# The first image's channel statistics shared between VectorE and ScalarE, and three early loads issued from another queue

## The chip, the core and the metric

One core of a Trainium2 chip runs the kernel. The metric is the device time of one execution in microseconds (us), the median of several. VectorE is called DVE in the profile, ScalarE is ACT, TensorE is PE (its weight loads PEld), GpSimd is POOL, and SyncE, which here only issues transfers, is SP.

## The reference, cut to what matters

The input `x` has shape (2, 512, 64, 64): two images of 512 channels. Two layers follow each other, each of the form `x = x + layer(_gn(x))`. The first is a deformable convolution (a projection by `in_w`, a depthwise 3x3 convolution with a layer norm and a GELU, offsets and masks from it, bilinear sampling, a projection by `out_w`), the second an attention layer with a batch norm at its end. Here only the first group norm matters:

```python
def _gn(v, G=32, eps=1e-5):
    B_, C_, H_, W_ = v.shape
    g = v.reshape(B_, G, C_ // G, H_, W_)
    m = jnp.mean(g, axis=(2, 3, 4), keepdims=True)
    s = jnp.var(g, axis=(2, 3, 4), keepdims=True)
    return ((g - m) / jnp.sqrt(s + eps)).reshape(v.shape)
```

Each image is thus read whole before anything of its first layer can start: mean and variance over 16 channels and all 4096 pixels.

## The kernel before, in words

The 512 channels are four blocks (`kb`, KB = 4) of 128 channels, one channel on each partition. An image's 4096 pixels are eight chunks (NCH = 8) of 512. The first layer goes over the 16 chunks of both images in turn (NSEQ = 16); the second layer follows when the first has ended.

**The head.** The four blocks of the first image are loaded into `img[0]` to `img[3]` (two of them lie in the room of `bt`, the other two in buffers called `img`), each block in two halves of 1 MB: the first half is issued by ACT, the second by SP (L649 and L650). Behind them SP issues the weights: `in_w` (L651), small vectors, `om_w`, `out_w`, `wv`, `wf`, and `edge` (L691). `image_stats(0)` (L703, called at L1148) then takes a `bn_stats` of each chunk of each block on DVE (L727), and a `bn_aggr` for each block (L729), which leave the mean and the variance of each channel in `mv`. `group_norm_steps` (L595) turns them into a scale and a bias for each channel: two small PE products with `gmat`, a few small DVE operations, and a square root on ACT (L611). Only then can `project(0)` normalize the first chunk into `xn` (L762) and multiply it by `in_w` (L772).

**The second image's statistics.** `image_stats(1)` is a generator that is advanced a step at a time between other work, by `more()`. It has room for three pieces of one chunk of one block each (256 KB): two in `early`, one in `xraw`. `refill()` (L710) issues loads for free room, on POOL (L714); the first three are issued at its first step, the others when a `bn_stats` has emptied a piece.

**The order after the head** is written out by hand (L1154 on, under `manual_schedule`): the instructions of an engine, and the transfers it issues, keep the order in which the code names them. On SP this is: eight stores of the projected first chunk (L780), then `border()` (L695), 16 stores of `edge` into the borders of both projected images (L698 with 68 rows, L699 with 64 rows), then two stores of `wc_part` (L1134, from `value_weights`, L1124), then the stores of the second projected chunk. `more()` at L1166, the first step of `image_stats(1)`, stands behind `border()` in the code. `wc_part` and the projected rows `xj` (L777, L778) share two buffers, so the first `xj` of the second chunk waits until the first `wc_part` has been stored. What stands outside the hand-written order (the loads, `image_stats(0)`) is placed by a scheduler that works with modelled times.

Of the kernel before, what the change touches and what calls it, by code (L numbers as in the profile page):

```python
# [10 lines left out]
F32 = mybir.dt.float32  # L11
I32 = mybir.dt.int32
AF = mybir.ActivationFunctionType
ALU = mybir.AluOpType
AX = mybir.AxisListType
# [3 lines left out]
P = 128  # L19
NB = 2  # L20
C = 512
KB = C // P
H = W = 64
S = H * W
# [7 lines left out]
CH = 512  # L32
NCH = S // CH
# [521 lines left out]
def window_path(  # L555
# [3 lines left out]
    nc = tc.nc  # L559
    x_v = t_in["x"].rearrange("n (cb p) h w -> n p cb (h w)", p=P)  # L560
# [34 lines left out]
    def group_norm_steps(mv, k, small, psum, result):  # L595

        p1 = psum.tile([P, CH], F32, tag="mm", name="gn_p1")
        nc.tensor.matmul(p1[:, : 2 * k], gmat, mv.rearrange("p k s -> p (k s)"), start=True, stop=True)
        yield
        gm = small.tile([P, k, 2], F32, name=f"gn_gm{k}")  # L600
        nc.vector.tensor_copy(gm.rearrange("p k s -> p (k s)"), p1[:, : 2 * k])
        d = small.tile([P, k], F32, name=f"gn_d{k}")
        nc.vector.tensor_sub(d, mv[:, :, 0], gm[:, :, 0])
        nc.vector.tensor_mul(d, d, d)
        yield
        p2 = psum.tile([P, CH], F32, tag="mm", name="gn_p2")
        nc.tensor.matmul(p2[:, :k], gmat, d, start=True, stop=True)
        yield
        var = small.tile([P, k], F32, name=f"gn_var{k}")
        nc.vector.tensor_add(var, gm[:, :, 1], p2[:, :k])  # L610
        nc.scalar.activation(var, var, AF.Sqrt, bias=eps)  # L611
        yield
        sc = small.tile([P, k], F32, name=f"gn_sc{k}")
        nc.vector.reciprocal(sc, var)
        bi = small.tile([P, k], F32, name=f"gn_bi{k}")
        nc.vector.scalar_tensor_tensor(bi, gm[:, :, 0], -1.0, sc, ALU.mult, ALU.mult)
        result += [sc, bi]
# [8 lines left out]
    with ExitStack() as l0:  # L626
# [3 lines left out]
        sm = l0.enter_context(tc.tile_pool(name="w0small", bufs=1))  # L630
        ps = l0.enter_context(tc.tile_pool(name="w0ps", bufs=4, space=PSUM))
# [11 lines left out]
        img = [bt.rearrange("p g q d -> p (g q d)")[:, h * S : (h + 1) * S] for h in range(2)]  # L643
# [59 lines left out]
        def image_stats(n):  # L703

            mv = sm.tile([P, KB, 2], F32, name="gn_mv")
            room = [early[:, 0], early[:, 1], io.tile([P, CH], F32, name="xraw")] if n else []
            pieces, ahead = deque((kb, h) for kb in range(KB) for h in range(NCH)), deque()


            def refill():  # L710
                while len(ahead) < 3 and pieces:
                    k2, h2 = pieces.popleft()
                    ahead.append(room[len(pieces) % 3])
                    nc.gpsimd.dma_start(ahead[-1], x_v[n, :, k2, h2 * CH : (h2 + 1) * CH])  # L714

            if n:
                refill()
                yield
            for kb in range(KB):
                st = sm.tile([P, NCH, 6], F32, name="gn_st")  # L720
                for h in range(NCH):
                    if n == 0:
                        t = img[kb][:, h * CH : (h + 1) * CH]
                    else:
                        refill()
                        t = ahead.popleft()
                    nc.vector.bn_stats(st[:, h, :], t)  # L727
                    yield
                nc.vector.bn_aggr(mv[:, kb, :], st.rearrange("p a b -> p (a b)"))  # L729
            yield  # L730
            result = []
            yield from group_norm_steps(mv, KB, sm, ps, result)
            sc, bi = result
            gn[n] = [sm.tile([P, KB], F32, name=f"gn_{k}{n}") for k in ("scale", "bias")]
            nc.vector.tensor_copy(gn[n][0], sc)
            nc.vector.tensor_copy(gn[n][1], bi)
# [400 lines left out]
        def output_bias():  # L1137
# [8 lines left out]
            yield  # L1146

        run(image_stats(0))  # L1148
        later, y, f = image_stats(1), Chain(sample, NSEQ), Chain(features, 2)

        def more():
            next(later, None)

        with tc.manual_schedule():  # L1154
# [59 lines left out]
            for i in range(NSEQ):  # L1214
# [11 lines left out]
                ahead, taps = (7, (9, 7, 6, 6)) if i else (0, (7, 7, 6, 6))  # L1226
# [8 lines left out]
    with ExitStack() as l1, tc.manual_schedule():  # L1235
# [78 lines left out]
        with ExitStack() as inner:  # L1314
            wk = inner.enter_context(tc.tile_pool(name="w1work", bufs=1))
            ps = inner.enter_context(tc.tile_pool(name="w1ps", bufs=1, space=PSUM))
# [562 lines left out]
            for n in range(NB):  # L1879
# [3 lines left out]
                for i in range(NCH // 2):  # L1883
                    if 0 < i < 3 or n and i == 0:
                        k = i + 1 if i else 1
# [164 lines left out]
```

## Time and profile before

| what | us |
|---|---|
| median of 3 runs (lowest, highest) | 3310.23 (3306.95, 3310.55) |
| the profiled execution's own time | 3315.49 |
| its span in the profile | 3313.6 |
| PE busy | 3154.1 (95%) |
| DVE busy | 2729.4 (82%) |
| ACT busy | 1343.0 (41%) |
| first normalization on ACT (L762) starts | 36.56 |
| first product with `in_w` on PE (L772) starts | 37.48 |

The profile is of one execution. In the timeline each row gives the start, the duration, the engine, the line, the operation, output and inputs, and in brackets the time for which the engine had been idle and what ended that. SPq and ACTq are the sequencers that issue transfers. In the chain of waits each piece is the work that ended last, in order of time. The table's last two rows say how long the core waits before its matrix work begins.

### The profile page before, as it was taken

The numbers are of one execution on the slowest core, as the hardware profiler recorded it, in microseconds if no ns is written. First come the engines' busy times: TensorE is split into PE (matmuls) and PEld (weight loads), VectorE is DVE, ScalarE is ACT, GpSimd is POOL, SyncE is SP. The second block draws the span as 40 slices with busy tenths as digits, with TensorE's granted clock in tenths as the row PEclk, the third lists the DMA queues.
The fourth block names the chain that finished last, engine by engine and source line by source line (L and its number), as shares of the span: only waits on it lengthen the run. The fifth ranks groups of instructions, "written<-read, shape, count | busy, mean of one in ns | idle before, by whom it ended". The sixth has DMA issues, their size and how long they took to land.

```text
span 3313.6 us, 38405 instructions
## 1 busy us (share of the span) xinstructions
PE 3154.1 (95%) x14207; PEld 2264.5 (68%) x14207; DVE 2729.4 (82%) x3907; ACT 1343.0 (41%) x1848; POOL 292.0 (9%) x420
## 2 busy tenths in 40 slices
PE   4899999999999899999999999999999999999993
PEld 2455556555655667787787877887777787787782
DVE  7999999999998678995876977968897796886875
ACT  2678887888786533203113112023311202203114
POOL 1100000000000001001001011000001101001022
PEclk9999999999999999999999999999999999999997
DMA  6345443444343368748657677657677758648689
GB/s 238 120 117 155 151 129 109 137 146 118 109 136 124 115 236 282 220 154 242 189 174 212 197 203 204 199 185 251 226 213 200 205 181 234 199 160 238 194 320 373
DMA packets 241236, 629.06 MB, mean 190 GB/s; under 512 B 28528, under 2 KB 45552, under 8 KB 240016
## 3 DMA queue, kind: packets, MB, share of 16 engines
q1 hardware_dynamic: 177952, 413.37, 37.8%
q0 software_dynamic: 51936, 179.86, 20.7%
q10 hardware_dynamic: 11152, 33.30, 2.7%
q8 instruction: 114, 1.87, 0.2%
q14 instruction: 82, 0.67, 0.1%
HBM read 406.61 MB, written 124.91 MB: 160 GB/s over the span
## 4 chain that ended last, share of the span: by engine, by line
PE 79%; DVE 10%; ACT 5%; DMA 3%; issue 1%; SPq 1%; POOL 0%; ACTq 0%; POOLq 0%; DVEq 0%
PE accy L1572 21%; PE accx L1572 16%; PE pa L976 7%; PE py L996 6%; PE pS L1454 6%; PE pq L772 6%; PE po L866 4%; PE pvy L1809 3%; PE pvx L1809 2%; PE pk L1890 2%; PE pb L957 2%; ACT bt L962 1%; DMA tot<-e 1%; DVE conv L806 1%; PE p_mean L822 1%
## 5 line engine op out<-in xcount | busy, mean ns | idle before, releaser
L1572 PE MATMUL accy<-tt,v 128*128 128x256 f32 x1944 | 579.0, 379 | 0.7 <-DVE ct L1638 0.6
L1459 ACT ACTIVATE e<-pS 128x1024 f32<-128x1024 f32 x256 | 248.6, 1021 | 748.5 <-PE pS L1454 744.2
L1572 PE MATMUL accx<-e,v 128*128 128x256 f32 x1728 | 453.3, 385 | 0.0
L1572 PE MATMUL accy<-e,v 128*128 128x256 f32 x1728 | 443.4, 379 | 0.0
L1572 PEld LDWEIGHTS accy<-tt,v 128*128 128x128 f32 x1944 | 368.7, 190 | 53.3 <-DVE tt L1530 2.2
L806 DVE SCALAR_TENSOR_TENSOR conv<-xn,L_conv_dw_w_sb,conv 128x504 f32<-128x504 f32 (+1 forms) x512 | 376.7, 744 | 30.5 <-ACT conv L798 14.7
L1572 PEld LDWEIGHTS accx<-e,v 128*128 128x128 f32 x1728 | 320.5, 190 | 116.3 <-issue 77.4
L1572 PEld LDWEIGHTS accy<-e,v 128*128 128x128 f32 x1728 | 328.3, 190 | 44.6
L1530 DVE TENSOR_TENSOR tt<-tt,e 128x512 f32<-128x512 f32 x432 | 298.8, 692 | 14.8
L1572 PE MATMUL accx<-tt,v 128*128 128x256 f32 x972 | 289.4, 379 | 1.3 <-DVE tt L1529 1.3
L1529 DVE TENSOR_TENSOR tt<-e 128x256 f32<-128x256 f32 x432 | 180.7, 418 | 133.0 <-PE accy L1572 131.0
L976 PEld LDWEIGHTS pa<-bt,patch 96*128 96x128 f32 x2048 | 248.3, 195 | 57.1 <-issue 39.2
L976 PE MATMUL pa<-bt,patch 96*128 96x128 f32 x2048 | 252.3, 280 | 7.5 <-issue 4.0
L1454 PE MATMUL pS<-q,keys 64*128 64x512 f32 x1024 | 255.5, 616 | 1.1 <-DVE vform L1827 0.8
L962 ACT COPY bt<-pb 96x1024 f32<-96x1024 f32 x120 | 226.0, 2024 | 52.6 <-PE pb L957 52.6
L772 PE MATMUL pq<-in_w,xn 128*128 128x512 f32 x512 | 234.1, 600 | 3.5 <-ACT xn L762 3.5
L996 PE MATMUL py<-dT,L_conv_out_w_sb 128*128 128x512 f32 x512 | 230.0, 593 | 0.0
L1577 ACT COPY u<-accx 128x256 f32<-128x256 f32 x54 | 20.1, 372 | 474.5 <-PE accx L1572 471.7
L866 PE MATMUL po<-om_w_pg,feat 128*128 128x432 f32 x512 | 210.3, 557 | 0.8 <-ACT feat L849 0.8
L987 ACT COPY dT<-pa 32x256 f32<-32x256 f32 x496 | 179.9, 363 | 67.8 <-PE pa L976 59.0
L1572 PEld LDWEIGHTS accx<-tt,v 128*128 128x128 f32 x972 | 184.4, 190 | 27.6 <-DVE tt L1529 2.5
L996 PEld LDWEIGHTS py<-dT,L_conv_out_w_sb 128*128 128x128 f32 x512 | 95.5, 190 | 114.3 <-issue 107.6
(289 smaller groups left out, 4386.7 us busy)
## 6 DMA issues: line engine op xcount, KB each, us to landing
v<-wv SPq DMA_DIRECT2D x420, 448.0 KB
tot<-e POOLq DMA_DIRECT2D x160, 512.0 KB, 6.8
patch<-xt SPq DMA_DIRECT2D x256, 192.0 KB
wv<-vform SPq DMA_DIRECT2D x48, 512.0 KB
v<-ww SPq DMA_DIRECT2D x54, 448.0 KB
wv<-vsum SPq DMA_DIRECT2D x48, 384.0 KB
xt<-xj SPq DMA_DIRECT2D x128, 128.0 KB
res<-in_x SPq DMA_DIRECT2D x64, 256.0 KB
```

Source lines behind the costliest of these rows:

```text
L772: nc.tensor.matmul(pq, xn[:, kb, 1 + 2 * t : 3 + 2 * t, :].rearrange("p r c -> p (r c)"), in_w[:, kb, :], start=(kb == 0), stop=(kb == KB ...
L806: nc.vector.scalar_tensor_tensor(dst, src, wt, dst, ALU.mult, ALU.add)
L866: nc.tensor.matmul(po[:, : 3 * GP], f[:, kb, t * P : (t + 1) * P], om_w[:, kb].rearrange("p a k g -> p (a k g)"), start=(kb == 0), stop=(k ...
L962: copy(bt[:SN].rearrange("s g q d -> s d (g q)")[:, d0 : d0 + 4, :], pb[:SN])
L976: nc.tensor.matmul(pa[:, p], xp[:SN, p, cb * P : (cb + 1) * P], bt[:SN, 4 * cb : 4 * cb + 4, PX * s + p, :], start=True, stop=True,)
L987: copy(dst, src)
L996: nc.tensor.matmul(py, out_w[:, kb, cb * P : (cb + 1) * P], dT[:, kb, :], start=(kb == 0), stop=(kb == KB - 1))
L1454: nc.tensor.matmul(p[:, a, :], keys[r, i, (2 * u + h) * P : (2 * u + h + 1) * P], c.q[r, qh, :], start=True, stop=True,)
L1459: nc.scalar.activation(e.rearrange("p a q -> p (a q)"), p.rearrange("p a q -> p (a q)"), AF.Exp)
L1529: nc.vector.tensor_sub(t[:, 0], x[:, 1], x[:, 3])
L1530: nc.vector.tensor_add(t[:, 1:3], t[:, 0].unsqueeze(1).to_broadcast([P, 2, HQ]), x[:, 0:3:2])
L1572: nc.tensor.matmul(out, v[:, blk, :], op, start=(first and g == 0), stop=(final and g == NG))
```

## The change

For the first image (n = 0) block 1 is left out of the loop on DVE. In its place ACT goes over the eight chunks of `img[1]` twice each: Identity with scale 1/4096, and Square with scale 4096^-0.5, both into scratch tiles in PSUM, with `accum_out`, which adds up each row of 512 values: 16 instructions give eight partial sums of the mean and eight of the mean square. Ahead of block 3's statistics DVE joins them: a sum over the eight parts, the square of the mean, and a subtraction. For the second image nothing of this applies; but its first three loads (256 KB each) are issued by SP in place of POOL, at the same place in the code: the first `more()`, behind `border()`.

```diff
                     k2, h2 = pieces.popleft()
                     ahead.append(room[len(pieces) % 3])
-                    nc.gpsimd.dma_start(ahead[-1], x_v[n, :, k2, h2 * CH : (h2 + 1) * CH])
+                    queue = nc.gpsimd if len(pieces) < KB * NCH - 3 else nc.sync
+                    queue.dma_start(ahead[-1], x_v[n, :, k2, h2 * CH : (h2 + 1) * CH])
 
             if n:
                 refill()
                 yield
+            by_scalar = 1 if n == 0 else KB
+            if n == 0:
+                acc = sm.tile([P, 2, NCH], F32, name="gn_acc")
+                for h in range(NCH):
+                    for k, (func, scale) in enumerate(((AF.Identity, 1.0 / S), (AF.Square, S ** -0.5))):
+                        p = ps.tile([P, CH], F32, tag="mm", name="p_sq")
+                        nc.scalar.activation(
+                            p, img[by_scalar][:, h * CH : (h + 1) * CH], func, scale=scale,
+                            accum_out=acc[:, k, h : h + 1]
+                        )
             for kb in range(KB):
+                if kb == by_scalar:
+                    continue
+                if n == 0 and kb == KB - 1:
+                    both = mv[:, by_scalar, :]
+                    nc.vector.tensor_reduce(both, acc, AX.X, ALU.add)
+                    nc.vector.tensor_mul(acc[:, 0, 0:1], both[:, 0:1], both[:, 0:1])
+                    nc.vector.tensor_sub(both[:, 1:2], both[:, 1:2], acc[:, 0, 0:1])
                 st = sm.tile([P, NCH, 6], F32, name="gn_st")
```

## Prediction

> **What bounds the kernel now.** I read the chain of waits of the first 120 us first, because the change touches nothing behind that. Columns: start, us, what.
>
> ```profile
> 1.66 17.45 DMA bt<-in_x
> 19.11 0.02 issue
> 19.14 2.49 DVE gn_st L727 x4
> 21.62 0.02 issue
> 21.65 0.38 DVE gn_mv L729
> 22.03 0.02 issue
> 22.05 4.86 DVE gn_st L727 x8
> 26.93 0.38 DVE gn_mv L729
> 27.34 4.86 DVE gn_st L727 x8
> 32.22 0.38 DVE gn_mv L729
> ...
> 71.88 4.94 DMA wvfc<-wc_part
> 76.82 0.02 issue
> 76.84 0.02 ACTq L778
> 76.86 0.04 issue
> 76.90 0.59 ACT xj L778
> 77.48 0.00 issue
> 77.48 0.02 ACTq L778
> 77.50 0.04 issue
> 77.54 0.59 ACT xj L778
> 78.13 0.54 ACT feat L832
> ```
>
> Two places matter. **The head**: from 19.14 to 32.60 DVE works without a break on blocks 1, 2 and 3; the end of that sets the first matrix product at 37.48. **The SP queue**: from 55.6 on the chain runs through the 16 border stores, then through the store of `wc_part`, whose landing at 76.8 frees the buffer for `xj`. ACT takes its work in order, so Square (L832) stands behind `xj`, and PE, which had run out of work at 71.2 (L772: 64.17 + 7.03), goes on only at 78.71. The timeline of SP shows what stands there:
>
> ```profile
> 69.37 1.92 SPq L698 DMA_DIRECT2D xt<-raw  x1
> 71.33 0.45 SPq L699 DMA_DIRECT2D xt<-raw  x1
> 71.88 2.34 SPq L1134 DMA_DIRECT2D wvfc<-wc_part  x2
> ```
>
> The hand-written order puts the three moved loads exactly between the last two of these rows. That SP keeps that order is seen in the trace: `edge` was ready for the border at 43.34 (L693: 42.92 + 0.42), SP sat waiting for `xj` 18.4 us between 44 and 55, and still issued all eight L780 before the first border store.
>
> **Part 1: transfers leave the head.** POOL issues the first pieces of the second image at 2.67 to 4.33, and in windows of 1 us its queue moves 0.79 MB between 5 and 18 us, beside the first image. From 18 to 25 us all queues together move about 0.415 MB per us, so 0.79 MB are 1.9 us. SP's queue had moved the second half of block 2 at 22.4 us; a release follows its last byte by about 1.4 us here (block 0's half: 11.2 and 12.67; block 1's: 17.5 and 19.11; block 3's: 25.1 and 26.4). So that half lands at 23.8 before and at 21.9 after; block 1's halves at 12.5 and 17.2, block 3's last at 24.5.
>
> **Part 2: DVE's chain.** Block 1's eight `bn_stats` and aggregate (5.3 us) go. What is late next is a load: DVE does block 0, then block 2's first half, then waits for its second half until 21.9. From there: four `bn_stats` 2.43, aggregate 0.41, end 24.74; the join; then block 3, which before began at 27.34. The join's operations have no row of their size: a reduction took 0.145 (L543, one column) to 0.277 (128 elements, L1787), a small subtraction 0.18 (L603), a small product 0.16, but 0.85 the first time (L604: one of 0.850, three near 0.161). Together 0.5 to 1.2. The slow first product is already in the chain at 33.69, so by these rows it would only move to the join; I take 0.5 net. Block 3 then starts at 25.24: **2.1 us earlier**. Ends: 2.6 if the join is hidden in a wait, 1.4 if it costs 1.2.
>
> **Part 3: ACT's new work.** Sixteen instructions of 128x512 with an accumulator into PSUM; no row shows just that. Square from SBUF to SBUF (L832) is 0.62, four in 2.19. With an accumulator there is L890: 1.15 for 1152 elements, and the reading of the accumulator (0.187) lets the next one start 1.15 after the first, so it hardly adds. Low end 0.55 each, high end the slowest row of this width (L798, 0.814) plus 0.187: 1.0 each. I take 0.62, by L832 and L890. Block 1's first half lands at 12.5, so eight end at 17.5, when the second half is there (17.2); all end at 22.4. DVE needs the sums at 24.74: covered by 2.3 us, and ACT had nothing else to do (idle 30.76 before L611 at 35.42). At 1.0 each ACT ends at 28.5, block 3 starts at 29.0 and the head is 1.7 us later than before. A table load took 1.283 (at 3.38, far ahead of the square root): another one would fall in the ACT idle time from 22.4 to 33. The Trainium skill speaks against this division of work (ScalarE: Activation LUTs, Rules for kernel authors: adding and multiplying belong on VectorE, and a switch of table sets is to be budgeted at some 2.7 us). With such a switch on the path the head would be 0.6 us later, in place of 2.1 earlier; the idle row says it is off the path.
>
> **Part 4: three loads on SP.** They stand in front of `wc_part`, so whatever they take goes onto the chain at 71.88. Nothing of it is hidden: PE is idle 7.5 us there, and Square's input was ready at 69.13. Issue alone is 3 x 0.45 = 1.35. By the bytes: 0.79 MB at 0.415 is 1.9; at the rate at which the two `wc_part` stores moved (0.52 MB in some 1.6 us) 2.4. By the slow border rows (1.92 for one) it would be 5.8, by the slowest (2.35) 7.05. Low end 0. I take **1.9**, because the queue is in order and bytes wait there, and a 128-row tile is spread like `wc_part`, not like the slow 68-row L698. One rule of the Trainium skill bears on that (DMA: Bandwidth & Descriptors, in the part on the number of engines: the largest divisor up to 16 of the row count): 68 rows would run on 4 engines and 64 on 16, which fits L698 beside L699; by it the loads pay like L699, and the sum would use 1.35 to 1.9. The same page (Issuing engines are not separate DMA queues) holds that the issuing engine matters only for issue time; by that, Part 4 would cost 1.35.
>
> The loads then land at about 75.5, 76.2 and 76.8 on the old clock, and DVE reads them at 77.39, 77.99 and 78.58: no wait, with 1.8 us to spare. If they came 2 us later, DVE would wait that long, and pieces 3 to 5 with it; `rstd` follows at 85.3 from the PE side, and DVE's own work ends at 85.89, so up to 1.9 us of that vanish behind part 4's delay. POOL loses three issues of 0.55 in its idle time: nothing. Weights behind the image arrive 1.9 us earlier (`in_w` landed at 28.98, PE needs it at 35.4): nothing late there. `edge` finishes moving at about 38.8, lands near 40.2, and DVE's L693 would come at 40.8: covered by 0.6.
>
> **Sum.** -2.1 in the head, +1.9 on SP: -0.2 us. From 78.7 to 111 the chain is PE, then ACT and DVE, all released by this point, so the sum goes through unchanged. Against the profiled execution (span 3313.6, time 3315.49, so 1.9 outside the span, untouched) that is 3315.3; that execution is 5.3 above the median of the runs, so against the median: **3310.0**.
>
> **Rivals.**
> A. *The loads do not stand in the way*: SP issues them directly behind the first image's loads, or the other transfer engines take them beside the border stores. Part 4 is 0, the sum -2.1: 3308.1. Against it: SP's order in the trace.
> B. *The SP queue becomes the price* (slower): each load is issued at the pace of L698, 1.77 to 2.35, because the queue ahead is full; 5.3 to 7.05 at 71.88, less 2.1: +3.2 to +5.0, 3313.4 to 3315.2. It outweighs the gain from 0.7 us for each load on. For it: SP's issues do stall there; against it: every L699 between them took 0.45 to 0.67 but one.
> C. *ACT is late for the join*: at 1.0 us for each instruction the head loses 1.7; with part 4, +3.6: 3313.8. DVE then waits at the join with block 3 behind it. Against it: the L832 and L890 rows.
>
> **How the numbers follow.** About 0.2% (6.6 us) is what a measurement of this kernel tells from no change. Chances: my forecast 0.57, A 0.14, B 0.17, C 0.08, and 0.04 for a gain I cannot see. None of the forecast and A passes 0.2% by its terms; B and C do so only at their ends (B with the head's gain lost as well: +7.05; C and B together: +8.8). So of B 0.05 and of C 0.02 go to slower; of A 0.02 and the unseen 0.04 to faster; the same 0.87. The range: low, the best head (-2.6) with part 4 at nothing is 3307.6, less 2 for the spread of medians (three runs span 3.6); high, part 4 at 5.8 with no gain is 3316.0.
>
> **What would show it.** Right: L727 of block 2 pauses until about 22, ACT ends its sixteen near 22.4, first L772 at about 35.4; three SP loads between L699 and L1134; `xj` released near 76.6; PE's idle time before L822 grows by about 2. Wrong: SP loads ahead of L780 (A); SP rows above 1.5 us for a load (B); DVE waiting for ACT before block 3 (C).

## The result, and the profile after

| | median of runs, us | lowest to highest | runs |
|---|---|---|---|
| before, same chip | 3311.11 | 3306.95 to 3317.07 | 22 |
| with the change | 3317.97 | 3312.09 to 3322.24 | 22 |

The medians lie 6.9 us apart; the ratio on record, over all runs, is 1.0016, with a 95% interval from 1.001 to 1.0022: slower by about 5.3 us (3.3 to 7.3). Two more comparisons of the same program below gave 1.0006 [0.9997, 1.0015] and 1.0007 [0.9998, 1.0016]. Weighted by the inverse square of their widths, the three make 1.0012 [1.0007, 1.0016], about 3.8 us. The forecast was -0.2 us and a median of 3310.0, with 3316.0 as the upper end of its range.

A single execution says little about a change of this size. The profiled one with the change has a span of 3314.7 us (own time 3316.83), and two other profiles of the same program (e5, e10) had 3307.2 and 3320.9. What can be compared is the first 200 us of each record, where the work is fixed and the differences are of one place each.

**The head.** First the timeline of DVE in the changed kernel (start, duration, engine, line, operation, output and inputs, and in brackets the idle time and what ended it):

```profile
21.32 2.47 DVE L745 BATCH_NORM_STATS2 gn_st<-img 128x6 f32<-128x512 f32 x4 [2.23 <-DMA img<-in_x]
...
24.23 4.85 DVE L745 BATCH_NORM_STATS2 gn_st<-img 128x6 f32<-128x512 f32 x8
29.11 0.37 DVE L747 BATCH_NORM_AGGREGATE gn_mv<-gn_st 128x2 f32<-128x48 f32 x1
29.40 0.11 DVE L735 TENSOR_REDUCE gn_mv<-gn_acc 128x2 f32<-128x16 f32 x1
29.55 0.73 DVE L736 TENSOR_TENSOR gn_acc<-gn_mv 128x1 f32<-128x1 f32 x1
30.31 0.85 DVE L737 TENSOR_TENSOR gn_mv<-gn_mv,gn_acc 128x1 f32<-128x1 f32 x1
...
32.06 0.87 DVE L603 TENSOR_TENSOR gn_d<-gn_mv,gn_gm 128x4 f32<-128x4 f32 x1
32.97 0.85 DVE L604 TENSOR_TENSOR gn_d<-gn_d 128x4 f32<-128x4 f32 x1
```

Block 2 pauses for its second half until 21.3, as forecast, and block 3 is done at 29.48, 3.1 us earlier than the 32.60 of before. But the scheduler put the join (L735 to L737) behind block 3, not in front of it, and four operations that write one or four elements for each channel take 0.73 to 0.87 us each. In the kernel before one of them was that slow. Its rows for the last two (timeline of DVE, before):

```profile
33.48 0.18 DVE L603 TENSOR_TENSOR gn_d<-gn_mv,gn_gm 128x4 f32<-128x4 f32 x1
33.69 0.85 DVE L604 TENSOR_TENSOR gn_d<-gn_d 128x4 f32<-128x4 f32 x1
```

The timeline of POOL, changed kernel:

```profile
29.32 3.60 POOL L665 COPY om_w_pg<-om_w_sb 128x432 f32<-128x432 f32 x4 [26.57 <-DMA om_w_sb<-in_om_w]
32.85 0.94 POOL L666 COPY om_b_pg<-om_b_sb 128x432 f32<-128x432 f32 x1
```

and the same view of the kernel before:

```profile
31.81 3.60 POOL L665 COPY om_w_pg<-om_w_sb 128x432 f32<-128x432 f32 x4 [27.48 <-DMA om_w_sb<-in_om_w]
```

POOL's copies of `om_w` start when that weight has landed. With the three loads gone from the head it lands 2.5 us earlier, so the copies now run beside the whole join. The first product with `in_w` comes at 36.62, only 0.86 us before the 37.48 of before.

**The SP queue.** The timeline of SP, changed kernel:

```profile
68.15 0.48 SPq L698 DMA_DIRECT2D xt<-raw  x1
68.68 1.56 SPq L699 DMA_DIRECT2D xt<-raw  x1
70.29 1.74 SPq L715 DMA_DIRECT2D early<-in_x  x2
72.07 0.42 SPq L715 DMA_DIRECT2D xraw<-in_x  x1
72.59 0.85 SPq L1152 DMA_DIRECT2D wvfc<-wc_part  x2
```

The last border store ends 1.5 us earlier than before (70.24, before 71.78), and from the first load to the store it is 2.30 us. The store of `wc_part` starts 0.7 us later than the 71.88 of before. PE restarts at 79.44 after an idle time of 9.11 (timeline of PE, bracket; the first row is the kernel before, the second the change):

```profile
78.71 5.87 PE L822 MATMUL p_mean<-feat,ones_c 128*128 128x512 f32 x8 [7.51 <-ACT feat L832]
79.44 6.06 PE L840 MATMUL p_mean<-feat,ones_c 128*128 128x512 f32 x8 [9.11 <-ACT feat L850]
```

**The clock behind it.** Busy times in stretches of 4 us, in the order PE, PEld, DVE, ACT, POOL; the next column is the granted clock, as a share of full speed. Before:

```profile
74.00:78.00 4.00, 0.00 (x0) 0.00 (x0) 3.86 (x7) 1.05 (x2) 0.00 (x0) 0.79 0.40 146
82.00:86.00 4.00, 4.00 (x9) 1.66 (x8) 2.11 (x4) 0.69 (x1) 2.40 (x3) 0.86 0.63 230
```

With the change:

```profile
74.00:78.00 4.00, 0.00 (x0) 0.00 (x0) 3.89 (x7) 0.34 (x1) 0.48 (x1) 0.50 0.57 203
82.00:86.00 4.00, 4.00 (x8) 1.77 (x7) 1.39 (x2) 0.46 (x1) 2.92 (x4) 0.72 0.70 242
```

The clock is at half rate from 74.0 to 84.2 with the change (10.2 us), from 76.3 to 83.1 before (6.8 us), and again from 138.8 for 13.7 us (before from 137.7 for 10.2 us). PE's work is 0.9 us later than in the record of before at 133 us and 1.5 us later at 191 us.

### The profile page after: what moved, and what is told of

Read it like the earlier page. It is cut to its first block, busy times and chain, and to the rows that moved or that the text cites. A ratio compares the mean times of both kernels' runs of the same rounds, so it can differ in the third digit from the quotient of the medians.

```text
span 3314.7 us, 38432 instructions
## 1 busy us (share of the span) xinstructions
PE 3149.9 (95%) x14207; PEld 2261.5 (68%) x14207; DVE 2727.0 (82%) x3901; ACT 1354.3 (41%) x1881; POOL 290.6 (9%) x417
## 3 DMA queue, kind: packets, MB, share of 16 engines
q1 hardware_dynamic: 178384, 414.16, 37.7%
```

## The experiments

Three theories. **S**: the place of the three loads on SP, in front of `wc_part`, is the price. **P**: DVE's small operations with two inputs in SBUF wait for POOL's copies, which eats the head's gain. **C** (rival): the new ACT instructions cost something by standing in the program (code, table, scratch), wherever their result is used. Ratios are to the kernel before on the same chip, each with its 95% interval; of each kernel there are 11 or 12 runs, of the kernel before 27 to 35.

**e1, statistics alone.**

```diff
-                    queue = nc.gpsimd if len(pieces) < KB * NCH - 3 else nc.sync
+                    queue = nc.gpsimd
```

> ScalarE takes block 1's statistics, but the three loads stay on POOL at the start. Theory S (the SP queue is the price): wc_part lands as early as the head allows, PE's idle time before L822 stays near 7.5 us, the head gains about 0.5 to 1 (the loads still share the image's bandwidth, 1.9 us), so 0 to 1 us faster than before. Theory C (the new ACT instructions cost something later, by their place in the program): about 5 us slower, as the whole change. Theory P (DVE's small operations wait for POOL's copies): the three join operations and L603, L604 show 0.7 to 0.9 each where they fall beside L665.

Measured 3314.62, ratio 1.0007 [0.9998, 1.0016]. The first product comes at 39.21, 1.7 us later than before, where up to 1 us earlier was expected: the loads' bytes are still in the head, so block 3 ends only 0.6 us earlier (31.98), and POOL's copies (from 31.92) again meet all four small operations (0.83 to 0.87 each). PE restarts at 78.99 after 6.06 us of idle time.

**e2, loads alone**: the three loads on SP, all statistics on DVE, no new ACT instructions.

```diff
-            by_scalar = 1 if n == 0 else KB
...
-                if kb == by_scalar:
-                    continue
```

> DVE does all four blocks, the first three loads stand on SP behind the border. Theory S: the head is at most 1 us earlier, PE's idle time before L822 is 9 to 9.5 us in place of 7.5, and the time is 2 to 6 us longer than before. Theory C: no change, since ACT's program is as before.

Measured 3316.57, ratio 1.0011 [1.0002, 1.002]. First product at 36.12 (1.36 us earlier than before, more than expected), `wc_part` at 73.22, restart at 80.47 (1.76 us later), idle time 10.63. The head's gain is there and the restart is late all the same: S.

**e3, the kernel before with sixteen idle ACT instructions**, whose sums nobody reads.

```diff
+                        nc.scalar.activation(
+                            p, img[1][:, h * CH : (h + 1) * CH], func, scale=scale,
+                            accum_out=acc[:, k, h : h + 1]
+                        )
```

> The kernel before, with the sixteen ACT instructions added whose sums nobody reads; DVE does all statistics, the loads stay on POOL. Theory C: about 5 us slower with the same head. Theory S: within 1 us of before, since they lie in ACT's idle time.

Measured 3315.72, ratio 1.0004 [0.9995, 1.0013]; first product 37.55, restart 78.77, -0.3 us at 191 us. C finds nothing here.

**e4, the change with the loads on POOL again, but behind its copies.**

```diff
-                    queue = nc.gpsimd if len(pieces) < KB * NCH - 3 else nc.sync
...
+                    queue = nc.gpsimd
+                    with tc.issue_after(om_last.ins) if len(pieces) >= KB * NCH - 3 else ExitStack():
```

> ScalarE's statistics as in the change; the three loads stay on POOL but are queued behind its copies L665 and L666, so they move at about 35 us, behind the image and ahead of the border. Theory S: PE's idle time before L822 is back near 7.5 us, PE starts L772 0.9 us earlier than before, the time is about 1 us less than before. Theory C: about 5 us slower than before. Theory P: the join and L603, L604 are slow as in the changed kernel, since the copies begin at 29.3 again.

Measured 3313.57, ratio 0.9998 [0.9989, 1.0007]. The loads are issued at 34.2 to 35.9, far from SP; `wc_part` goes out at 70.84 and PE restarts at 77.76, 1.7 us before the change's 79.44. S again.

**e5, the change once more.** An unchanged program, beside e6, e7 and e8.

> The change as it is, once more, so that the other three kernels of this group have it beside them on the same chip. First product at 36.6, PE idle some 9.1 us in front of the first p_mean, +0.9 us against the kernel before at 85 us and at 133 us. Over many runs 3 to 7 us above the kernel before, if the first comparison holds.

Measured 3314.01, ratio 1.0006 [0.9997, 1.0015]. In its record POOL's copies met L603 and L604 but not the join (0.16 each), so its first product came at 35.52; from the first load to the store it was 3.18 us, and the restart came at 79.31. A head 1.1 us better than that of the first record bought 0.13 us. Against the expected 3 to 7 us above the kernel before, this comparison gives about 2.

**e6, the join in front of block 3**, where its words place it.

```diff
-                    nc.vector.tensor_sub(both[:, 1:2], both[:, 1:2], acc[:, 0, 0:1])
+                    joined = nc.vector.tensor_sub(both[:, 1:2], both[:, 1:2], acc[:, 0, 0:1])
...
+                    with tc.issue_after(joined.ins) if (n, kb) == (0, KB - 1) else ExitStack():
```

> The change with the join held in front of block 3, where its three operations run at about 24.3, before POOL's copies of om_w start at 29.3. Theory P (DVE's operations with two SBUF inputs wait for those copies): the join's product and subtraction take about 0.16 each instead of 0.73 and 0.85, the head is 1.3 us shorter than the change's (first product near 35.3), gn_p's first operations L603 and L604 stay near 0.85. Rival (the first such operation is slow wherever it stands): the product in front of block 3 takes 0.7 to 0.85 as well, and the head gains at most 0.2. Theory S (the end of the SP queue sets the restart of PE, whatever the head does): the wc_part store stays near 72.6 and the restart at p_mean near 79.4, so the time from there on is that of the change, within 0.3 us; if the head is handed on instead, the restart comes 1.3 us earlier.

Measured 3314.03, ratio 1.0008 [0.9999, 1.0017]. The timeline of DVE:

```profile
24.23 0.16 DVE L736 TENSOR_TENSOR gn_acc<-gn_mv 128x1 f32<-128x1 f32 x1
24.43 0.16 DVE L737 TENSOR_TENSOR gn_mv<-gn_mv,gn_acc 128x1 f32<-128x1 f32 x1
...
31.12 0.85 DVE L604 TENSOR_TENSOR gn_d<-gn_d 128x4 f32<-128x4 f32 x1
```

The first product of its kind is not slow: at 24.2, with POOL idle, it takes 0.16. L604, beside POOL's copies (29.25 to 33.7), takes 0.85. That is P, and against what the prediction said of L604. The first product with `in_w` is at 34.91, 2.6 us before that of the kernel before, and the restart is still at 79.14: S.

**e7, the copies of `om_w` and `om_b` on ACT.**

```diff
-            nc.gpsimd.tensor_copy(om_w[:, kb], om_w0[:, kb].rearrange("p (a g k) -> p a k g", a=3, k=NP))
-        nc.gpsimd.tensor_copy(om_b, om_b0.rearrange("p (a g k) -> p a k g", a=3, k=NP))
...
+            nc.scalar.copy(om_w[:, kb], om_w0[:, kb].rearrange("p (a g k) -> p a k g", a=3, k=NP))
+        nc.scalar.copy(om_b, om_b0.rearrange("p (a g k) -> p a k g", a=3, k=NP))
```

> The change with the copies of om_w and om_b on ScalarE, so that POOL does nothing beside gn_p. Theory P: the join's product, its subtraction, L603 and L604 take about 0.16 each (2.7 us less in sum), less what the copies delay on ScalarE in front of the square root and the first xn (up to 0.5): first product near 34.2. Rival (slow wherever they stand): 0.7 to 0.85 for each again, first product no earlier than 36.6. The loads still stand on SP, so PE's idle time in front of p_mean stays at 9 us or more.

Measured 3312.18, ratio 1.0002 [0.9992, 1.0011]. The join, L603 and L604 take 0.16 each, as P has it. The gain is given back on ACT, by more than I expected: its copies run from 29.74 to 33.3 and delay the square root's table load, so L614 waits 2.29 us and the first product is at 36.55, not 34.2. Idle time of PE 10.56, restart 80.83.

**e8, that, and the loads on ACT's queue** in the middle of the first projection; **e15** is the same program again.

```diff
-                    queue = nc.gpsimd if len(pieces) < KB * NCH - 3 else nc.sync
+                    queue = nc.gpsimd if len(pieces) < KB * NCH - 3 else nc.scalar
...
                 p0(2)
+                if t == 1:
+                    more()
                 f0(8)
             border()
-            more()
```

> As the kernel with the copies on ScalarE, and the three loads are issued from ScalarE's queue after the second product group (about 46 us) in place of SP. Theory S: nothing stands in front of wc_part, which is issued some 2.3 us earlier than in the change; PE's idle time in front of p_mean is 7.5 us or less, and the restart comes at 76 to 77.5 instead of 79.4: 2 to 3 us less than the change at 133 us, 1 to 2 less than the kernel before. Rival (the queue is not the price, the bytes are): the restart stays within 0.5 us of the change's, since the same bytes move before it.

> The kernel with the copies and the loads on ScalarE's queue, again on this chip, since it alone was below the kernel before (ratio 0.9989). If that is its own, -1.7 us or so at 133 us again and a median 1 to 4 us below the kernel before; if it was chance, within 1 us of it.

Measured 3309.67, ratio 0.9989 [0.998, 0.9998], and 3313.21, ratio 0.9998 [0.9989, 1.0007]. The three loads take 1.3 us of ACT's queue in a gap at 46 us; `wc_part` goes out at 70.46 and 70.60, PE restarts at 77.51 and 76.97. The expected 2 to 3 us against the change came (1.8 to 4.2 us at the restart, by the three records of it); whether this version beats the kernel before is open, the two comparisons together make 0.9994 [0.9987, 1.0000].

**e9 and e12** were to hold POOL's copies until `gn_bias` is written, e9 with the loads as in e8, e12 in the kernel before.

```diff
-        for kb in range(KB):
-            nc.gpsimd.tensor_copy(om_w[:, kb], om_w0[:, kb].rearrange("p (a g k) -> p a k g", a=3, k=NP))
...
+        with tc.issue_after(gn_last[0].ins):
+            for kb in range(KB):
+                nc.gpsimd.tensor_copy(om_w[:, kb], om_w0[:, kb].rearrange("p (a g k) -> p a k g", a=3, k=NP))
```

> ScalarE keeps the sums of block 1; POOL's copies of om_w and om_b wait until gn_bias is written, so that neither engine stands in the group norm's way; the three loads go out from ScalarE's queue after the second product group. By theories S and P the two prices of the change are gone and its gain stays: join, L603 and L604 at 0.16 each, first product near 34.3 (3 us before that of the kernel before), wc_part issued in front of 70, restart at p_mean near 75 to 76, -3 to -4 us at 133 us against the kernel before; 3 to 4 us below its median. If only the queue matters: about -1.7 at 133 us, as with the copies on ScalarE.

> The kernel before, with nothing of the change but POOL's copies of om_w and om_b held until gn_bias is written. Theory P: L604 takes 0.16 in place of 0.85 and L616 0.16 in place of 0.36, so the first product comes 0.7 to 0.9 us earlier (36.6), and -0.7 to -0.9 us reach 133 us; below what the runs can tell. If the slow product is slow as the first of its kind, nothing moves.

Measured 3313.94, ratio 1.0001 [0.9992, 1.001], and 3314.04, ratio 1.0 [0.9991, 1.0009]. Both missed, because the edit did nothing: an order of issue between two engines makes no wait, and POOL copied at 29.67 and 31.77 as ever. Neither says anything of P. e12 has the instructions of the kernel before in the same order on every engine, so it is a second record of it, and shows what one record is worth: restart 77.63 against 78.71, -0.9 us at 191 us.

**e10, the change a third time.**

> The change as it is, on this chip. The records of its two earlier profiles agree on +0.9 to +1.0 us at 133 us, while the two comparisons gave +5.3 and some +1.4 us. If the change's own price is what the records show up to there, a third comparison lies between 0 and +4; if there is a further price that comes behind 133 us each time, it lies near +5 again.

Measured 3316.56, ratio 1.0007 [0.9998, 1.0016]. That is about 2.3 us, inside the 0 to 4 named for the price that the records show. First product at 36.42, restart at 81.16 (idle 10.80), +3.5 us at 191 us.

**e11, the loads on SP behind `wc_part`** in place of in front of it: the smallest edit that tests S.

```diff
             border()
-            more()
...
                     next(products)
                     next(products)
+                    more()
```

> The change with the three loads still on SP, but behind the two stores of wc_part in place of in front of them. Theory S: the stores are issued at about 70 and land at about 75, xj is released 2.3 to 3 us earlier than in the change, the restart comes at 76.5 to 77.2 and PE's idle time is 7.5 us or less: -1 to -2 us at 133 us against the kernel before. The loads then land near 79, and DVE waits 1 to 2 us for the first of them, with nothing late behind it. Rival (the bytes on the queues are the price, not the place): the stores still land at 77 or later.

Measured 3314.92, ratio 1.0002 [0.9993, 1.0011]. The timeline of SP:

```profile
70.05 2.33 SPq L1152 DMA_DIRECT2D wvfc<-wc_part  x2
72.44 1.28 SPq L715 DMA_DIRECT2D early<-in_x  x2
```

The store leads, PE restarts at 76.89 with an idle time of 6.24, and 191 us is reached 1.4 us before the record of the kernel before. Same bytes, same queue, other order: the place is the price. The forecast wait of DVE for the first load did not come (it read it at 76.84 without a wait).

**e13 and e14, the copies truly held**: POOL first copies `gn_bias` into a spare tile, so its copies wait for it by a data dependence. e13 has the loads as in e8, e14 is the kernel before with this alone.

```diff
+        hold = sm.tile([P, KB], F32, name="hold")
+        held = nc.gpsimd.tensor_copy(hold, gn[0][1])
+        with tc.issue_after(held.ins):
+            for kb in range(KB):
+                nc.gpsimd.tensor_copy(om_w[:, kb], om_w0[:, kb].rearrange("p (a g k) -> p a k g", a=3, k=NP))
```

> As the kernel meant to be best, but now POOL reads gn_bias into a spare tile ahead of its copies, so that they start only when gn_bias is written; the loads go out from ScalarE's queue. Theory P: join, L603 and L604 at 0.11 to 0.19 each, ScalarE free for the square root: first product near 35.3 (2.1 us before that of the kernel before), and with the queue free in front of wc_part -2.5 to -3.5 us at 133 us. Rival (slow as the first of their kind): 0.65 to 0.87 again and a first product no earlier than 36.5.

> The kernel before with the same hold on POOL's copies and nothing else. Theory P: L604 0.16 in place of 0.85, L616 0.16 in place of 0.36: first product near 36.6 in place of 37.5, and -0.5 to -1.9 us at 133 us (the spread that the records of an unchanged program show there is 0.9). POOL's copies end near 41: nothing needs them before 79.

Measured 3311.96, ratio 0.9997 [0.9988, 1.0006], and 3314.17, ratio 1.0006 [0.9997, 1.0015]. The timeline of DVE in e13:

```profile
30.03 0.16 DVE L733 TENSOR_TENSOR gn_acc<-gn_mv 128x1 f32<-128x1 f32 x1
...
31.48 0.16 DVE L604 TENSOR_TENSOR gn_d<-gn_d 128x4 f32<-128x4 f32 x1
```

The same instructions take 0.16 behind block 3 too, as soon as POOL is still: P is shown. The first product is at 34.44 in e13 and 36.31 in e14. But the copies now run beside DVE's convolution. Both are slower for it: the four copies take 4.57 us in place of 3.60, and the convolution's first three operations 3.48 in place of 2.30 (e5, e6). Timelines of POOL and of PE in e13:

```profile
33.68 4.57 POOL L1168 COPY om_w_pg<-om_w_sb 128x432 f32<-128x432 f32 x4
...
61.94 1.12 PE L837 MATMUL p_mean<-conv,ones_c 128*128 128x512 f32 x2 [1.76 <-DVE conv L821]
```

So of 3.0 us gained in the head 1.3 are left when PE runs out of work (69.9, before 71.2). That loss falls into idle time: the store goes out 2.8 us earlier than before, and the restart comes 2.85 us earlier. At 191 us e13 is 2.4 us ahead of that record, the best of all, and its runs can't be told from those of the kernel before.

**All records side by side** (us; the first store of `wc_part` on SP, PE's restart at `p_mean` and the idle time ahead of it, the half-rate stretches at the restart and at 139, the shift of PE at 191 us against the record of before):

| kernel | first product | store | restart | idle | half rate | at 191 |
|---|---|---|---|---|---|---|
| before | 37.48 | 71.88 | 78.71 | 7.51 | 6.8, 10.2 | 0 |
| e12 | 37.44 | 70.83 | 77.63 | 6.47 | 6.8, 10.2 | -0.9 |
| e3 | 37.55 | 71.89 | 78.77 | 7.38 | 6.8, 10.2 | -0.3 |
| e14 | 36.31 | 70.74 | 76.71 | 4.91 | 6.8, 13.7 | -0.4 |
| e1 | 39.21 | 73.24 | 78.99 | 6.06 | 6.8, 13.7 | +1.0 |
| e4 | 37.08 | 70.84 | 77.76 | 6.96 | 6.8, 10.2 | -0.4 |
| e8 | 36.57 | 70.46 | 77.51 | 7.21 | 6.8, 10.2 | -1.7 |
| e15 | 36.27 | 70.60 | 76.97 | 6.98 | 6.8, 10.2 | -1.2 |
| e9 | 36.97 | 71.86 | 79.09 | 8.40 | 6.8, 10.2 | -0.2 |
| e11 | 36.93 | 70.05 | 76.89 | 6.24 | 6.8, 10.2 | -1.4 |
| e13 | 34.44 | 69.10 | 75.86 | 5.92 | 6.8, 10.2 | -2.4 |
| **loads on SP in front:** | | | | | | |
| change | 36.62 | 72.59 | 79.44 | 9.11 | 10.2, 13.7 | +1.5 |
| e5 | 35.52 | 73.00 | 79.31 | 10.07 | 10.2, 13.7 | +1.6 |
| e10 | 36.42 | 73.58 | 81.16 | 10.80 | 13.7, 13.7 | +3.5 |
| e2 | 36.12 | 73.22 | 80.47 | 10.63 | 10.2, 13.7 | +2.4 |
| e6 | 34.91 | 72.61 | 79.14 | 9.81 | 13.7, 13.7 | +2.2 |
| e7 | 36.55 | 73.70 | 80.83 | 10.56 | 10.2, 10.2 | +2.0 |

From the first product to the store it is 36.0 to 37.7 us with the loads in front (mean 37.1) and 33.1 to 34.9 without (34.1): **3.0 us**, with no overlap. The runs show a difference of that order: the ratios of the six below the line, weighted, make 1.0010 [1.0006, 1.0013], those of e1, e3, e4, e8, e9 and e11 to e15 make 1.0000 [0.9997, 1.0003]; the difference is about 3.2 us, and 2.2 us without the first comparison of the change.

## Why the prediction was wrong, step by step

- **Part 1 and its consequence, "Weights behind the image arrive 1.9 us earlier ...: nothing late there" (said behind part 4).** This step failed. They do arrive earlier (`om_w` by 2.5 us), nothing is late, but something is early: POOL's copies, which now stand beside the join and the group norm. The prediction asked only who waits for the weights, not what they set off.
- **Part 2, the head 2.1 us earlier.** The load, the pause until 21.3 and block 3 were right or better (its end 3.1 us earlier). The step that failed is "The slow first product is already in the chain at 33.69, so by these rows it would only move to the join". L604 was not slow as the first of its kind but because of POOL (e6, e7, e13, e14). The join, which the sum has in front of block 3, also stood behind it, beside the copies; in front of it, it takes 0.16 for each product (e6). In the record of the change four operations pay 0.73 to 0.87 in place of 0.16: 2.7 us lost, against 0.9 before (L604 and L616). In the six records with the loads out of the head, the sums on ACT and the join and the copies as in the change (the change, e4, e5, e9, e10, e11) the first product is at 36.6 in the mean, against 37.5 in the three without any of it (before, e3, e12): 0.9 us. With the copies held in both, e14 against e13, it is 36.31 against 34.44: 1.9 us, so the term was sized rightly for a head without POOL.
- **Part 3, ACT.** Right: one every 0.61 us, ended at 21.4 (forecast 22.4), the second table load (1.28 us at 21.53) in idle time. Rival C is out.
- **Part 4, three loads on SP, 1.9.** Right in kind, too small: 2.30 to 3.18 us from the first load to the store in the three records of the change, and 3.0 from the first product to the store. Rival A is out. Rival B named the queue as the price, which is right, but not the pace: the first two loads took 1.7 to 2.6 us together, the third 0.42. The 1.35 from issue time alone is too small as well. Nor is the slow row that of a 68-row store: in the change an L699 of 64 rows took 1.56 and the L698 ahead of it 0.48 (the rows at 68.68 and 68.15). One reading for this part was wrong: the 18.4 us of SP's waiting "between 44 and 55" are the sum of five waits and cannot all lie in 11 us; the order of SP's rows, on which the argument rests, stands.
- **The sum.** -0.9 and +3.0, each from its larger set of records, make +2.1 at the store of `wc_part`. The three records of the change alone have -1.3 at the first product (36.19 in the mean against 37.49 in before, e12 and e3) and +2.8 from there to the store, which make +1.5 (73.06 against 71.53). At the restart it is 79.97 against 78.37: +1.6 in place of -0.2.
- **"The sum goes through unchanged."** This failed too. At 191 us the three records of the change stand at +2.2 in the mean, the three without at -0.4: 2.6 us, which is 1.0 us more than at the restart. At 133 us the difference is 2.0; these first 0.4 are within the scatter of the records. The other 0.6 come between 133 and 191 us, and there the clock is the cause as far as the records go: the seven kernels with 13.7 us at half rate at 139 lose 0.5 to 1.0 us between these two places, the ten with 10.2 us lose 0.0. All six kernels that idle 9.1 us or more ahead of the restart get three or four half-rate windows of 3.4 us there, all eleven that idle 8.4 or less get two; and five of the six, against two of the eleven, have one more at 139. No run sets the idle time and nothing else, so the limit between 8.4 and 9.1 is only what these records show. The Trainium skill has the rule (TensorE: Matmul & The Clock Gate, What's actually happening): a free-running window of 3413 ns, half rate after an idle one. The lengths here, 6.8, 10.2 and 13.7, are two, three and four of these.
- **What stays open.** The records account for 2.6 us of 3.8 [2.4, 5.3]. That the first comparison gave 5.3 and the next two about 2 is not explained; their intervals overlap, so it can be chance. Half-rate windows of 3.4 us also fall singly, most of them between 200 and 1260 us, and differ in number and place from execution to execution. The three records of the change (e5, the first, e10) have 17.1, 27.3 and 34.1 us at half rate between 200 and 3200 us and spans of 3307.2, 3314.7 and 3320.9. The six kernels below the line have 28.4 us of this in the mean (17 to 41), the eleven above it 25.1 (17 to 38): no run here ties their number to the change.

## What to carry to other kernels

When transfers leave a queue or a stage, list what lands earlier in consequence and what work that sets off, on every engine, and lay that beside the chain. A load moved behind a queue of stores stands in front of the next store: put it behind the one that frees a buffer (e11), or in a gap of another queue (e8). A row that is five times as slow as its kind is a question to the other engines' rows at that time, before it is a property of the instruction.

## What the runs showed of the hardware

- A DVE operation with two inputs in SBUF, of one to four elements for each partition, takes 0.16 us alone and mostly 0.62 to 0.87 us beside POOL's copies, of which four take 3.60 us; the sum over 16 elements with one input (L735) takes 0.11 either way. POOL pays in turn beside DVE's convolution: four copies in 4.57 us in place of 3.60 (e13). The Trainium skill states this (SBUF — State Buffer, Who interferes with whom): a DVE instruction with two SBUF inputs contends with a GpSimd instruction that reads SBUF. The rows above agree with it.
- An Identity or Square of 128x512 on ACT with an accumulator takes 0.58 us and its reading 0.19, which overlaps: one every 0.61 us.
- Three loads of 256 KB take 2.20 to 3.08 us to issue on SP behind the border stores (the change, e5, e10), 1.75 behind `wc_part` (e11), and 1.30 on ACT's queue at 46 us (e8). The first two transfers behind the border are slow whichever they are: loads 1.74 to 2.62 us, the stores of `wc_part` 1.39 to 2.85; behind the three loads the same two stores take 0.85 to 0.88.
- The runs of the kernel before spread over 9 to 14 us on each chip, and three profiles of the change over 13.7 us of span.
